# Seven products in place of eight for a graph layer's weights, with the result turned back

## The chip, the core and the metric

The kernel runs on one core of a Trainium2 chip. The metric is the time of one execution on the device in microseconds (us), as the median of several runs. The engines go by the profile's names: PE (TensorE) multiplies matrices and also turns tiles (transposes), DVE (VectorE), ACT (ScalarE) and POOL (GpSimd) work on rows and columns, SP (SyncE) starts the transfers. Matmuls write to PSUM, a small memory of eight banks; everything else is in SBUF. Each engine takes its instructions in a fixed order, the one in which the program issues them, and waits where the data of the next one is not there.

## The reference

The input `x` holds 128 graphs of 64 nodes with 256 features, 8192 rows in all, and `adj` is a 64 x 64 matrix. Four layers follow each other, each with a layer norm and relu ahead and a residual add behind it:

```python
h = jnp.maximum(_layernorm(x, axis=-1), 0.0)
x = x + _L0_gnn_ref(h, adj, ...)      # two graph products with weights, then four window LSTMs
...
x = x + _L1_gnn_ref(h, adj, ...)      # normalised graph product, two weights with batch norms
...
x = x + _L2_gnn_ref(h, L2_gnn_W, adj, L2_gnn_bias)
...
x = x + _L3_gnn_ref(h, adj, L3_gnn_Wqkv, L3_gnn_Wo)   # causal attention over 64 nodes, one head
```

The change is in layer 2, whose three graphs are the diagonal, the upper and the lower part of `adj`, each with a weight of 256 x 256:

```python
def _L2_gnn_ref(x, W, adj, bias):
    adj_0 = jnp.diag(jnp.diagonal(adj))
    adj_1 = jnp.triu(adj, k=1)
    adj_2 = jnp.tril(adj, k=-1)
    h = jnp.einsum('bjf,kfo->kbjo', x, W)
    out = (jnp.einsum('ij,bjo->bio', adj_0, h[0]) + jnp.einsum('ij,bjo->bio', adj_1, h[1])
           + jnp.einsum('ij,bjo->bio', adj_2, h[2]))
    return out + bias[None, None, :]
```

All is in 32-bit floating point.

## The kernel before

The 8192 rows are cut into 16 tiles of 512 rows (`SUP`), each of which lies in SBUF as four groups of 128 rows (`Q`, index `q`), two graphs a group. Layers 0 and 1 run first, over all tiles, since the batch norms need sums over all rows. They leave their result feature-major: features on the 128 partitions in two chunks (`KC`, index `c`), rows along the free axis. The last stage, with layers 2 and 3, is the one that is changed. It takes the tiles in eight pairs of an even tile A and an odd tile B, and the same order of work comes back in every pair.

That order is written by hand. The function `rest` (L1186) holds all the steps of one tile, and each step is entered in a list with a nominal time, `at(t, step, ...)`. `PERIOD` is 52.5 nominal us, and each pair's times are counted from its own start. The list is sorted by time and the steps are issued in that order (at the end of the function), so the nominal times set the order on every engine, and nothing more. A step whose data is late holds up all that stands behind it on its engine. Steps may have times far ahead of the pair's start and so be done within the pair before.

The steps of one tile, in order, with the engine that does each:

- `load` (SP) fetches the rows saved after layer 0. `affine` (L1205, DVE) applies the batch norm's scale and shift in place to the feature-major tile, 128 x 512 for each chunk. `turn` (L1221, PE) transposes to rows, eight transposes a tile, and `turned` (L1224, DVE) adds the residual: `x2`.
- `norm` for layer 2: `stats` (L1235 and L1236, DVE), `root` (L1240 on DVE adds the epsilon, L1241 on POOL raises to the power -1/2), `shift` (L1244, DVE) and `relu` (L1248, ACT): `h2`. Then `biased` (L1261, POOL) adds the layer's bias, spread over all partitions, to `x2`, in four instructions.
- `graphs3` (L1273, PE) multiplies `h2` by the three graphs. It makes `ag`, feature-major, 3 x 512 columns for each of two chunks. A tile has four events of this kind. Each takes two PSUM banks, one for each graph of a group; ACT copies one of them to SBUF and DVE the other (both L1278).
- `weigh` (L1285, PE) is the weight product. For each group of 128 rows it takes 128 x 128 pieces of `ag` as stationary operand and the weights `wl2` as moving one, 256 columns, in 3 x 2 matmuls. A tile has 24 of them. The result has rows on the partitions. `weighed` (L1291, DVE) adds `x2`, which gives `x3`.
- `norm` for layer 3 with the same functions, then `h3` (L1298, PE) and `h3_copy` (L1302, DVE) turn it feature-major: `h3T`.
- Attention: `qsum` (L1313, DVE, four differences), `qproduct` (L1326, PE), `qcopy` (L1330, ACT) and `qadd` (L1333, DVE) make the query side with seven products over halves in place of eight; `hv` (L1350, PE) and `hv_copy` (L1354, ACT) make the values, and `scores` (L1360, PE) the scores. `masked` (L1365, DVE), `largest` (L1370, DVE) and `exps` (L1373, ACT) are the softmax. `turn_e` (L1381, PE), `turned_e` (L1385 and L1386, DVE), `attend` (L1391, PE) and `attended` (L1396, DVE) close the layer, and the rows go out over SP. The last pair has other times and takes the query product directly.

PSUM is one pool of eight banks of 128 x 512 in this stage, and `bank()` gives the next one.

The form in seven products is already in other layers. A product of 2 x 2 blocks is made of seven products of sums of blocks (Strassen's form, in Winograd's variant). `weight_sum` (L309, POOL) makes the four sums of the weights once, `OF` (L297) says which block or sum of the weights belongs to product 1 to 7:

```python
A11, A12, A21, A22, S1, S2, S4 = range(7)
S3 = A21
OF = (None, A11, A12, S4, A22, S1, S2, S3)
...
op(*(w[:, m] for m in ((S1, A21, A22), (S2, S1, A11), (S3, A11, A21), (S4, A12, S2))[k]))
```

Of the kernel before, what the change touches and what calls it, by code (L numbers as in the profile page):

```python
# [20 lines left out]
def kernel(ctx: ExitStack, tc: tile.TileContext, a: dict, out: bass.AP):  # L21
# [615 lines left out]
    def at(t, fn, *args):  # L637
        events.append((t, len(events), fn, args))
# [259 lines left out]
    with tc.tile_pool(name="pz", bufs=1, reuse_waits="tile") as pz:  # L898
# [235 lines left out]
        late = ctx.enter_context(tc.tile_pool(name="late", bufs=1, side="right", reuse_waits="tile"))  # L1134
        adj4 = load_const("adj4", parts_d, [P, 4, P], late)
        adj3, smask = adj4[:, 0:3, :], adj4[:, 3, :]
        wl2 = [weight(f"wl2_{k}", a["W"][k], late) for k in range(3)]
        bl2 = row_bcast("bl2", a["bias"], D, late)
        wqk = late.tile([P, KC, D], F32, tag="wqk", name="wqk")
        aqk = late.tile([P, 7, P], F32, tag="aqk", name="aqk")  # L1140
        wvo = late.tile([P, KC, D], F32, tag="wvo", name="wvo")
        wqkv = weight("wqkv", a["Wqkv"], late)
        wo = weight("wo", a["Wo"], late)

        with tc.tile_pool(name="tp", bufs=2, reuse_waits="tile") as tp_:
            tp.append(tp_)
            emit(1e9)
# [29 lines left out]

    PERIOD, HALF = 52.5, SUP // 2  # L1180
    NP = NS // 2
    with tc.tile_pool(name="pc", bufs=2, reuse_waits="tile") as pc, \
            tc.tile_pool(name="pc1", bufs=1, reuse_waits="tile") as pc1:
        events = []

        def rest(s, at, only_pair, t_T, t_n, t_G, t_W, t_h, t_QH, t_S, t_soft, t_E, t_O, end):  # L1186
# [39 lines left out]
            def norm(src, tag, halves, t_rows, t_relu):  # L1226

                def new():
                    v["st"] = pc.tile([P, Q, 6], F32, tag="ln_st", name="ln_st", bufs=4)
                    v["mv"] = pc.tile([P, Q, 2], F32, tag="ln_mv", name="ln_mv", bufs=4)  # L1230
                    v["rn"] = pc.tile([P, 2, Q], F32, tag="ln_rn", name="ln_rn", bufs=4)
                    v[tag] = pc.tile([P, Q, D], F32, tag=tag, name=tag)

                def stats(q):
                    nc.vector.bn_stats(v["st"][:, q, :], v[src][:, q, :])  # L1235
                    nc.vector.bn_aggr(v["mv"][:, q, :], v["st"][:, q, :])  # L1236

                def root(qs):
                    rn = v["rn"][:, 0, qs]
                    nc.vector.tensor_scalar_add(rn, v["mv"][:, qs, 1], EPS)  # L1240
                    nc.gpsimd.tensor_tensor(rn, rn, mhalf[:, : qs.stop - qs.start], ALU.pow)  # L1241

                def shift(qs):
                    nc.vector.scalar_tensor_tensor(v["rn"][:, 1, qs], v["mv"][:, qs, 0], -1.0,  # L1244
                                                   v["rn"][:, 0, qs], op0=ALU.mult, op1=ALU.mult)

                def relu(q):
                    nc.scalar.activation(v[tag][:, q, :], v[src][:, q, :], AF.Relu,  # L1248
                                         bias=v["rn"][:, 1, q : q + 1], scale=v["rn"][:, 0, q : q + 1])

                at(t_rows[0] - 0.01, new)
                for q in range(Q):
                    at(t_rows[q // 2] + 0.6 * (q % 2), stats, q)
                for k, qs in enumerate((q2s(0), q2s(1)) if halves else (slice(0, Q),)):
                    at(t_relu[k] - 1.5, root, qs)
                    at(t_relu[k] - 0.1, shift, qs)
                    for q in range(qs.start, qs.stop):
                        at(t_relu[k] + 0.6 * (q - qs.start), relu, q)

            def biased(q):  # L1260
                nc.gpsimd.tensor_add(v["x2"][:, q, :], v["x2"][:, q, :], bl2)  # L1261

            def graphs3(c, k):

# [12 lines left out]
                    to = v["ag"][:, c, :, 2 * k * P : (2 * k + 2) * P]  # L1277
                    copy(to.rearrange("p k (q n) -> p q k n", q=2)[:, :, :, b * T : (b + 1) * T], half[b])  # L1278

            def weigh(k, q):  # L1280
                if q == 0:
                    v["W"] = two(bank())
                for n in range(3 * KC):
                    c, m = divmod(n, 3)
                    nc.tensor.matmul(v["W"][:, q, :], v["ag"][:, c, m, ts(2 * k + q, P)],  # L1285
                                     wl2[m][:, c, :], start=(n == 0), stop=(n == 3 * KC - 1))

            def weighed(k):
                if k == 0:
# [29 lines left out]
            def qproduct(name, j):  # L1319
                new = ("q", name) not in v  # L1320
                if new:
                    v["q", name] = bank()[:, :HALF]
                if "qk" not in v:
                    v["qk"] = pc1.tile([P, KC, SUP], F32, tag="qk", name="qk")
                x_ = (b_(0, 0), b_(1, 0), b_(1, 1), *(v["t"][:, k] for k in (4, 1, 2, 3)))[j - 1]
                nc.tensor.matmul(v["q", name], aqk[:, OF[j], :], x_, start=new,  # L1326
                                 stop=(name, j) in (("a", 4), ("b", 3), ("c", 2)), skip_group_check=True)
# [84 lines left out]
                at(t_T + 0.1 * k + 0.01, turned, k)  # L1412
            if first_:
                norm("x2", "h2", True, (t_T + 0.455, t_T + 1.8), (t_T + 3.2, t_T + 4.6))
                for q in range(Q):
                    at(t_T + 7 + 0.7 * q, biased, q)
            else:
                norm("x2", "h2", False, (t_n, t_n + 1.2), (t_n + (11.9 if s % 2 and s > 1 else 4.1),))
                for q in range(Q):
                    at(t_n + (18 if s % 2 else 10.5) + 0.7 * q, biased, q)  # L1420
# [47 lines left out]
        for i in range(NP):  # L1468
            t0, first_, end = PERIOD * i, i == 0, i == NP - 1

            def at(t, fn, *args, t0=t0):
                events.append((t0 + t, len(events), fn, args))

            rest(2 * i, at, i, -8.6 if first_ else -40.2, -38.3, 0, (7.0, 12.6), 29.0, 32.6, 40.0, 42.7,
                 46.3 if end else 48.46, 50.4 if end else 50.85, False)
            if first_:
                at(-7.6, weight_product, 2, wo, wvo)
                for k in range(8):
                    at(3.0 + 0.5 * k, qk_weights, k)
            rest(2 * i + 1, at, i, -3.0 if first_ else -27.6, 1.5 if first_ else -25.4, 12.3 if first_ else 3.5, (17.8, 26.5), 39.1,  # L1480
                 (42.0, 45.4, 48.7, 49.6, 52.1) if end else 42.0, 46.7 if end else 48.9,
                 49.5 if end else 59.5, 53.0 if end else 64.7, 53.8 if end else 75.6, end)
        for _, _, fn, args in sorted(events, key=lambda e: e[:2]):
            fn(*args)
    new_banks()
# [38 lines left out]
```

## Time and profile before

| what | value |
|---|---|
| median of 3 runs (lowest to highest) | 1876.81 us (1876.74 to 1877.57) |
| the profiled execution | 1876.78 us |
| its span | 1875.1 us |
| PE busy | 1853.9 us, 99% of the span |
| DVE, ACT, POOL busy | 1129.4, 925.7, 645.4 us |
| one period of the last stage | 50.88 us |
| of that PE, DVE, ACT, POOL busy | 50.88, 36.58, 20.23, 10.09 us |
| weight product L1285 | 768 matmul records |

The profile is of one execution. A 32-bit matmul appears as two records, so the 24 matmuls of 16 tiles are 768. The chain of waits is followed from the last instruction back to whatever let each step start. An engine's share of the chain is thus the part of the time that it set itself. A timeline gives start and length of each instruction or of several alike in a row, and in square brackets how long the engine stood idle before it and what ended that.

### The profile page before, as it was taken

To read this page: it belongs to the slowest core of one execution; us is meant where nothing else is said; L and a number is where in the kernel's file an instruction comes from. 1 tells how busy PE (TensorE), PEld (TensorE's weight loads), DVE (VectorE), ACT (ScalarE), POOL (GpSimd) and SP (SyncE) were. 2 spreads that over 40 slices of the span, in tenths; PEclk is the share of its full clock that TensorE was granted. 3 is DMA by queue.
4 is the path that set the end of the run, shared out by engine and by line. 5 is a ranking of instruction groups with operands and counts; after the bars stand their busy time and mean duration, and the time that the engine had idled before them with its cause. 6 is when DMAs were issued, how large, how long until landed. Compare 5 with 4: busy or idle time off the path is not lost.

```text
span 1875.1 us, 19841 instructions
## 1 busy us (share of the span) xinstructions
PE 1853.9 (99%) x7080; PEld 1168.8 (62%) x7080; DVE 1129.4 (60%) x2254; ACT 925.7 (49%) x1594; POOL 645.4 (34%) x553
## 2 busy tenths in 40 slices
PE   8999999999999999999999999999999999999999
PEld 7997444444445666666444444566444788888887
DVE  6775777634546435445633333588876776667674
ACT  6776666534435334433533333378685434433442
POOL 4451422443424433422442222267353412211220
PEclk9999999999999999999999999999999999999999
DMA  4110001000001000000000000243200111111101
GB/s 146 57 57 1 1 1 29 16 1 0 1 0 45 1 0 1 1 1 1 23 0 0 1 0 0 102 132 116 71 1 2 44 46 46 35 46 46 46 23 34
DMA packets 50642, 54.86 MB, mean 29 GB/s; under 512 B 3184, under 2 KB 45936, under 8 KB 50544
## 3 DMA queue, kind: packets, MB, share of 16 engines
q1 hardware_dynamic: 50096, 53.30, 8.9%
q8 instruction: 56, 0.92, 0.2%
q14 instruction: 42, 0.34, 0.1%
q10 hardware_dynamic: 448, 0.30, 0.0%
HBM read 36.55 MB, written 17.04 MB: 29 GB/s over the span
## 4 chain that ended last, share of the span: by engine, by line
PE 93%; DVE 3%; POOL 1%; ACT 1%; DMA 1%; issue 1%; SPq 0%; ACTq 0%; DVEq 0%; POOLq 0%
PE ps L686 34%; PE ps L692 19%; PE ps L1285 8%; PE ps L930 5%; PE ps L1047 4%; PE ps L1350 3%; PE ps L392 3%; PE ps L402 3%; PE ps L1326 2%; PE ps L431 2%; PE ps L1273 2%; PE ps L1360 2%; PE ps L1391 1%; PE ps L623 1%; PE ps L1298 1%; PE ps L579 1%
## 5 line engine op out<-in xcount | busy, mean ns | idle before, releaser
L708 DVE TENSOR_TENSOR gate<-gate,ps 128x512 f32<-128x512 f32 (+2 forms) x378 | 223.9, 620 | 449.0 <-PE ps L692 367.7
L686 PE MATMUL ps<-tx,wih 128*128 128x512 f32 (+2 forms) x996 | 441.2, 541 | 1.9 <-ACT gate L711 1.0
L686 PE MATMUL ps<-hT,wih 128*128 128x512 f32 (+2 forms) x756 | 338.5, 541 | 0.0
L711 ACT COPY gate<-ps 128x512 f32<-128x512 f32 (+2 forms) x252 | 134.5, 534 | 378.4 <-PE ps L692 325.4
L686 PEld LDWEIGHTS ps<-tx,wih 128*128 128x128 f32 x996 | 188.4, 190 | 188.2 <-issue 128.2
L704 ACT ACTIVATE gate<-gate,lbias 128x512 f32<-128x512 f32 (+2 forms) x252 | 216.7, 860 | 160.0 <-DVE gate L708 160.0
L692 PE MATMUL ps<-h,whh 128*128 128x512 f32 (+2 forms) x576 | 256.6, 527 | 0.0
L686 PEld LDWEIGHTS ps<-hT,wih 128*128 128x128 f32 x756 | 143.6, 190 | 141.6 <-issue 79.4
L692 PE MATMUL ps<-th,whh 128*128 128x512 f32 (+2 forms) x432 | 192.5, 527 | 0.0
L731 POOL TENSOR_TENSOR gate<-gate 128x1024 f32<-128x1024 f32 (+2 forms) x36 | 71.9, 2019 | 297.5 <-ACT gate L704 297.5
L1285 PE MATMUL ps<-wl,ag 128*128 128x256 f32 x768 | 172.1, 380 | 0.0
L692 PEld LDWEIGHTS ps<-h,whh 128*128 128x128 f32 x576 | 109.4, 190 | 100.2 <-issue 76.5
L1285 PEld LDWEIGHTS ps<-wl,ag 128*128 128x128 f32 x768 | 143.4, 190 | 20.2 <-ACT ag L1278 1.8
L731 POOL TENSOR_TENSOR cell<-gate 128x1024 f32<-128x1024 f32 (+2 forms) x36 | 79.4, 2225 | 174.8 <-ACT gate L704 174.8
L1241 POOL TENSOR_TENSOR ln_rn<-ln_rn,mhalf 128x4 f32<-128x4 f32 (+1 forms) x33 | 32.8, 995 | 300.8 <-DVE ln_rn L1240 300.3
L692 PEld LDWEIGHTS ps<-th,whh 128*128 128x128 f32 x432 | 82.1, 190 | 75.2 <-issue 57.4
L1248 ACT ACTIVATE h<-x,ln_rn 128x256 f32<-128x256 f32 x128 | 68.2, 593 | 103.3 <-DVE ln_rn L1244 103.3
L731 POOL TENSOR_TENSOR cell<-gate,cell 128x1024 f32<-128x1024 f32 (+2 forms) x31 | 62.8, 2044 | 110.2 <-ACT gate L704 110.2
L711 DVE COPY gate<-ps 128x512 f32<-128x512 f32 (+2 forms) x126 | 78.6, 624 | 20.8 <-PE ps L692 20.8
L704 ACT ACTIVATE gate<-ps,lbias 128x512 f32<-128x512 f32 (+2 forms) x126 | 79.6, 631 | 3.8 <-PE ps L692 1.0
L736 ACT ACTIVATE gate<-cell 128x1024 f32<-128x1024 f32 (+2 forms) x72 | 68.0, 951 | 26.1 <-POOL cell L731 26.1
L648 DVE TENSOR_TENSOR tx<-hT,tx 128x512 f32<-128x512 f32 (+2 forms) x70 | 57.7, 825 | 13.8 <-PE ps L686 10.2
(236 smaller groups left out, 2933.8 us busy)
## 6 DMA issues: line engine op xcount, KB each, us to landing
xt<-in_x_dram SPq DMA_DIRECT2D x30, 512.0 KB, 4.2
x1d<-xt SPq DMA_DIRECT2D x16, 512.0 KB, 3.0
x<-x1d SPq DMA_DIRECT2D x16, 512.0 KB, 4.9
out_dram<-x SPq DMA_DIRECT2D x15, 512.0 KB, 3.0
wih<-in_WihT_dram SPq DMA_DIRECT2D x16, 256.0 KB, 4.8
whh<-in_WhhT_dram SPq DMA_DIRECT2D x12, 256.0 KB, 4.8
xt<-in_x_dram SPq DMA_DIRECT2D x6, 128.0 KB, 3.2
wl<-in_W_dram SPq DMA_DIRECT2D x3, 256.0 KB, 3.6
```

Source lines behind the costliest of these rows:

```text
L648: yield nc.vector.tensor_sub(t[k], *((b[1][0], b[0][0]), (b[1][1], t[0]), (b[1][1], b[1][0]), (b[0][1], t[1 % len(t)]))[k])
L686: nc.tensor.matmul(wide(p_[:, :N]), wih[0][:, OF[k], gi, :], x_, start=first_, stop=(j == 0), skip_group_check=True)
L692: nc.tensor.matmul(p_[:, :N], whh[0][:, OF[k], gi, :], h_, start=False, stop=True, skip_group_check=True)
L704: nc.scalar.activation(to, r[bank_][:, :N] if bank_ else to, fn, bias=lbias[:, l, m : m + 1])
L708: nc.vector.tensor_add(slot(n, hc), slot(n, hc), r[bank_][:, :N])
L711: op(slot(n, hc), r[bank_][:, :N])
L731: fn(*((t["G"] if isinstance(t, dict) and "G" in t else st["c"])[:, n, :, : st["N"]] for t in tiles))
L736: nc.scalar.activation(o_, c, AF.Tanh)
L930: nc.tensor.matmul(r[name], con["w1"][:, OF[j], g, :], x_, start=new, stop=(name, j) in (("a", 4), ("b", 3), ("c", 2)), skip_group_check=True)
L1047: nc.tensor.matmul(banks[name], w2[:, OF[j], k, :], x_, start=(new and k == 0), stop=(k == 1), skip_group_check=True)
L1248: nc.scalar.activation(v[tag][:, q, :], v[src][:, q, :], AF.Relu, bias=v["rn"][:, 1, q : q + 1], scale=v["rn"][:, 0, q : q + 1])
L1285: nc.tensor.matmul(v["W"][:, q, :], v["ag"][:, c, m, ts(2 * k + q, P)], wl2[m][:, c, :], start=(n == 0), stop=(n == 3 * KC - 1))
```

## The change

Layer 2's weight product is taken the other way round and in seven products. The weights become the stationary operand and `ag` the moving one, in two halves of 256 columns (rows of the tile), so that the result is feature-major, 2 x 2 blocks: output chunk `o` by half `n`. A tile then has 7 x 3 matmuls of 256 columns. Tile 0 takes a direct product with the same operands, 24 matmuls (`gdirect`).

The steps that come with it: `gsum` makes the four sums of blocks of `ag`, 128 x 768 each, on POOL, two of them in place. `gevict` (ACT) brings four products from PSUM to SBUF and adds the bias, which is a column per output chunk in this layout; `gadd` (DVE) adds the other three from PSUM. `turn_back` (PE) transposes the result to rows, eight transposes, and `weighed` then adds `x2` as before. `biased` goes. The weights `wl2` are loaded in four pieces instead of three, with four weight sums on POOL.

PSUM is split into a pool of three banks for the products (those of the queries too) and one of five for the rest. The differences `qsum` move from DVE to POOL. In `norm` the shift of two operands on DVE is replaced by a product with -1 on DVE and a small product on POOL. Many nominal times change, among them the next tiles' turn (A -40.2 to -14.5, B -27.6 to -37.2) and B's end of the attention (64.7 to 67.35, 75.6 to 79.5).

```diff
-        wl2 = [weight(f"wl2_{k}", a["W"][k], late) for k in range(3)]
-        bl2 = row_bcast("bl2", a["bias"], D, late)
+        wl2 = late.tile([P, 7, 3, P], F32, tag="wl2", name="wl2")
+        for o in range(2):
+            for c in range(2):
+                nc.sync.dma_start(wl2[:, 2 * o + c], a["W"].rearrange(
+                    "m (c p) (o n) -> o c p m n", c=2, o=2)[o, c])
+        bl2 = load_const("bl2", a["bias"].rearrange("(c p) -> p c", p=P), [P, KC], late)
...
+        for k in range(4):
+            if k != 2:
+                at(B + 60 + 5.16 * k, weight_sum, wl2, k)
...
+    new_banks(abc=3, psum=5)
...
-                    rn = v["rn"][:, 0, qs]
+                    rn, nm = v["rn"][:, 0, qs], v["rn"][:, 1, qs]
                     nc.vector.tensor_scalar_add(rn, v["mv"][:, qs, 1], EPS)
+                    nc.vector.tensor_scalar_mul(nm, v["mv"][:, qs, 0], -1.0)
                     nc.gpsimd.tensor_tensor(rn, rn, mhalf[:, : qs.stop - qs.start], ALU.pow)
-
-                def shift(qs):
-                    nc.vector.scalar_tensor_tensor(v["rn"][:, 1, qs], v["mv"][:, qs, 0], -1.0,
-                                                   v["rn"][:, 0, qs], op0=ALU.mult, op1=ALU.mult)
+                    nc.gpsimd.tensor_mul(nm, nm, rn)
...
-            def biased(q):
-                nc.gpsimd.tensor_add(v["x2"][:, q, :], v["x2"][:, q, :], bl2)
...
-            def weigh(k, q):
-                if q == 0:
-                    v["W"] = two(bank())
-                for n in range(3 * KC):
-                    c, m = divmod(n, 3)
-                    nc.tensor.matmul(v["W"][:, q, :], v["ag"][:, c, m, ts(2 * k + q, P)],
-                                     wl2[m][:, c, :], start=(n == 0), stop=(n == 3 * KC - 1))
+            def g_(c, n):
+                return v["ag"][:, c, :, ts(n, HALF)]
+
+            def gsum(k):
+                if k == 0:
+                    v["t2"] = late.tile([P, 3 * KC, D], F32, tag="wT", name="tg")
+                t1, t2 = v["t2"][:, 0:3], v["t2"][:, 3:6]
+                if k == 0:
+                    nc.gpsimd.tensor_sub(t1, g_(0, 1), g_(0, 0))
+                elif k == 1:
+                    nc.gpsimd.tensor_sub(g_(0, 1), g_(1, 1), g_(0, 1))
+                elif k == 2:
+                    nc.gpsimd.tensor_add(t2, g_(0, 1), g_(0, 0))
+                else:
+                    nc.gpsimd.tensor_sub(g_(1, 0), g_(1, 0), t2)
+
+            def gproduct(name, j):
+                new = ("g", name) not in v
+                if new:
+                    v["g", name] = bank("abc")[:, :HALF]
+                x_ = (g_(0, 0), g_(1, 0), g_(1, 1), g_(1, 0), v["t2"][:, 0:3] if j == 5 else None,
+                      v["t2"][:, 3:6] if j == 6 else None, g_(0, 1))[j - 1]
+                for m in range(3):
+                    nc.tensor.matmul(v["g", name], wl2[:, OF[j], m, :], x_[:, m], start=new and m == 0,
+                                     stop=m == 2 and (name, j) in (("a", 4), ("b", 3), ("c", 2)),
+                                     skip_group_check=True)
...
+            def gevict(o, n, name):
+                if "y2" not in v:
+                    v["y2"] = late.tile([P, KC, 3 * D], F32, tag="wqkv", name="y2")
+                nc.scalar.activation(w_(o, n), v["g", name], AF.Identity, bias=bl2[:, o : o + 1])
+
+            def gadd(o, n, name):
+                nc.vector.tensor_add(w_(o, n), w_(o, n), v["g", name])
+
+            def turn_back(k):
+                v["W"] = two(bank())
+                for q in range(2):
+                    for c in range(KC):
+                        nc.tensor.transpose(v["W"][:, q, ts(c, P)], v["y2"][:, c, ts(2 * k + q, P)], ident)
...
-                nc.vector.tensor_sub(t[:, k], *(None, (b_(0, 1), b_(0, 0)), (b_(1, 1), t[:, 1]),
+                nc.gpsimd.tensor_sub(t[:, k], *(None, (b_(0, 1), b_(0, 0)), (b_(1, 1), t[:, 1]),
                                                 (b_(1, 1), b_(0, 1)), (b_(1, 0), t[:, 2]))[k])
...
-                    v["q", name] = bank()[:, :HALF]
+                    v["q", name] = bank("abc")[:, :HALF]
...
+            if first_:
+                for k in range(4):
+                    at(t_W[k], gdirect, k // 2, k % 2)
+            else:
+                for t, (name, j) in zip(t_W, (("c", 2), ("a", 1), ("b", 5), ("a", 6), ("b", 3), ("a", 7), ("a", 4))):
+                    at(t, gproduct, name, j)
+                for t, fn, *args in ((1, gevict, 0, 0, "a"), (2, gevict, 1, 1, "b"), (3, gevict, 0, 1, "a"),
+                                     (6, gevict, 1, 0, "a"), (4, gadd, 0, 1, "b"), (5, gadd, 1, 1, "a")):
+                    at(t_W[t] + 1.35, fn, *args)
+                at(t_W[1] + 1.8, gadd, 0, 0, "c")
+                for k in range(4):
+                    at(t_sums[k], gsum, k)
             for k in range(2):
-                for q in range(2):
-                    at(t_W[k] + 2.6 * q, weigh, k, q)
-                at(t_W[k] + 5.3, weighed, k)
-            norm("x3", "h3", False, (t_W[0] + 5.8, t_W[1] + 5.8), (t_W[1] + 8.8,))
+                at(t_Y[k], turn_back, k)
+                at(t_Y[k] + 0.5, weighed, k)
+            norm("x3", "h3", False, (t_Y[0] + 0.7, t_Y[1] + 0.7), (t_relu3,))
```

The nominal times of a pair, as they are in the changed version (in the order of `rest`'s arguments; the old ones are in the listing above):

```diff
+            rest(2 * i, at, i, -8.6 if first_ else -14.5, -12.5, 0,
+                 (7.0, 9.6, 12.2, 14.8) if first_ else (7.0, 8.3, 9.6, 10.9, 12.2, 13.5, 16.1),
+                 (3.3, 5.2, 7.1, 9.0), (17.4, 19.15) if first_ else (19.15, 17.4), 23.56, 26.1, 31.4, 40.0, 42.7,
+                 46.3 if end else 48.46, 50.4 if end else 50.85, False)
...
+            rest(2 * i + 1, at, i, -3.0 if first_ else -37.2, 1.5 if first_ else -35.8,
+                 12.3 if first_ else 3.5, (17.85, 19.6, 20.9, 22.2, 23.5, 24.8, 29.65),
+                 (16.0, 17.0, 18.0, 22.0) if first_ else (12.3, 14.2, 16.1, 22.0), (32.2, 30.95), 35.3, 39.1,
+                 (42.0, 45.4, 48.7, 49.6, 52.1) if end else 42.0, 46.7 if end else 48.9,
+                 49.5 if end else 59.5, 53.0 if end else 67.35, 53.8 if end else 79.5, end)
```

More of the change, by code (lines that the diff above doesn't have):

```diff
@@ L1184, with rest @@
         events = []
-        def rest(s, at, only_pair, t_T, t_n, t_G, t_W, t_h, t_QH, t_S, t_soft, t_E, t_O, end):
+        def rest(s, at, only_pair, t_T, t_n, t_G, t_W, t_sums, t_Y, t_relu3, t_h, t_QH, t_S, t_soft, t_E, t_O, end):
             first_, v = s == 0, {}
@@ L1249, in relu @@
                                          bias=v["rn"][:, 1, q : q + 1], scale=v["rn"][:, 0, q : q + 1])
-                at(t_rows[0] - 0.01, new)
+                at(min(t_rows) - 0.01, new)
                 for q in range(Q):
@@ L1255, in norm @@
                     at(t_relu[k] - 1.5, root, qs)
-                    at(t_relu[k] - 0.1, shift, qs)
                     for q in range(qs.start, qs.stop):
                         at(t_relu[k] + 0.6 * (q - qs.start), relu, q)
-            def biased(q):
-                nc.gpsimd.tensor_add(v["x2"][:, q, :], v["x2"][:, q, :], bl2)
             def graphs3(c, k):
@@ new lines, in gdirect, with w_ @@
+            def gdirect(n, o):
+                v["g", o] = bank("abc")[:, :HALF]
+                for c in range(KC):
+                    for m in range(3):
+                        nc.tensor.matmul(v["g", o], wl2[:, 2 * o + c, m, :], g_(c, n)[:, m],
+                                         start=(c == 0 and m == 0), stop=(c == KC - 1 and m == 2))
+                gevict(o, n, o)
+            def w_(o, n):
+                return v["y2"][:, o, ts(n, HALF)]
+            def gevict(o, n, name):
+                if "y2" not in v:
+                    v["y2"] = late.tile([P, KC, 3 * D], F32, tag="wqkv", name="y2")
+                nc.scalar.activation(w_(o, n), v["g", name], AF.Identity, bias=bl2[:, o : o + 1])
@@ L1288, in weighed @@
+            def gadd(o, n, name):
[3 more added lines that the diff above has]
+                for q in range(2):
+                    for c in range(KC):
+                        nc.tensor.transpose(v["W"][:, q, ts(c, P)], v["y2"][:, c, ts(2 * k + q, P)], ident)
             def weighed(k):
-                if k == 0:
+                if "x3" not in v:
                     v["x3"] = pc.tile([P, Q, D], F32, tag="x3", name="x3", bufs=4)
@@ L1414, in rest @@
                 norm("x2", "h2", True, (t_T + 0.455, t_T + 1.8), (t_T + 3.2, t_T + 4.6))
-                for q in range(Q):
-                    at(t_T + 7 + 0.7 * q, biased, q)
-            else:
-                norm("x2", "h2", False, (t_n, t_n + 1.2), (t_n + (11.9 if s % 2 and s > 1 else 4.1),))
-                for q in range(Q):
-                    at(t_n + (18 if s % 2 else 10.5) + 0.7 * q, biased, q)
+            else:
+                norm("x2", "h2", False, (t_n, t_n + 1.2), (t_n + (4.1 if s == 1 else 8.9 if s % 2 else 7.5),))
             for k in range(4):
                 at(t_G + 0.8 * k, graphs3, *((k % 2, k // 2) if first_ else (k // 2, k % 2)))
+            if first_:
[10 more added lines that the diff above has]
+                    at(t_sums[k], gsum, k)
             for k in range(2):
-                for q in range(2):
-                    at(t_W[k] + 2.6 * q, weigh, k, q)
-                at(t_W[k] + 5.3, weighed, k)
-            norm("x3", "h3", False, (t_W[0] + 5.8, t_W[1] + 5.8), (t_W[1] + 8.8,))
+                at(t_Y[k], turn_back, k)
+                at(t_Y[k] + 0.5, weighed, k)
+            norm("x3", "h3", False, (t_Y[0] + 0.7, t_Y[1] + 0.7), (t_relu3,))
             for c in range(KC):
@@ L1472, in at @@
                 events.append((t0 + t, len(events), fn, args))
-            rest(2 * i, at, i, -8.6 if first_ else -40.2, -38.3, 0, (7.0, 12.6), 29.0, 32.6, 40.0, 42.7,
+            rest(2 * i, at, i, -8.6 if first_ else -14.5, -12.5, 0,
+                 (7.0, 9.6, 12.2, 14.8) if first_ else (7.0, 8.3, 9.6, 10.9, 12.2, 13.5, 16.1),
+                 (3.3, 5.2, 7.1, 9.0), (17.4, 19.15) if first_ else (19.15, 17.4), 23.56, 26.1, 31.4, 40.0, 42.7,
                  46.3 if end else 48.46, 50.4 if end else 50.85, False)
@@ L1477 @@
                 at(-7.6, weight_product, 2, wo, wvo)
+                at(17.0, weight_sum, wl2, 2)
                 for k in range(8):
-                    at(3.0 + 0.5 * k, qk_weights, k)
-            rest(2 * i + 1, at, i, -3.0 if first_ else -27.6, 1.5 if first_ else -25.4, 12.3 if first_ else 3.5, (17.8, 26.5), 39.1,
+                    at(20.5 + 0.5 * k, qk_weights, k)
+            rest(2 * i + 1, at, i, -3.0 if first_ else -37.2, 1.5 if first_ else -35.8,
+                 12.3 if first_ else 3.5, (17.85, 19.6, 20.9, 22.2, 23.5, 24.8, 29.65),
+                 (16.0, 17.0, 18.0, 22.0) if first_ else (12.3, 14.2, 16.1, 22.0), (32.2, 30.95), 35.3, 39.1,
                  (42.0, 45.4, 48.7, 49.6, 52.1) if end else 42.0, 46.7 if end else 48.9,
-                 49.5 if end else 59.5, 53.0 if end else 64.7, 53.8 if end else 75.6, end)
+                 49.5 if end else 59.5, 53.0 if end else 67.35, 53.8 if end else 79.5, end)
         for _, _, fn, args in sorted(events, key=lambda e: e[:2]):
```

## Prediction

> **What bounds the kernel now.** I read first the engines' shares, then the chain that ended last, then the windows of three consecutive periods of the last stage (a period is one pair of tiles), then the timelines of DVE, ACT and POOL inside one of them.
>
> ```profile
> PE 1853.9 (99%) x7080; PEld 1168.8 (62%) x7080; DVE 1129.4 (60%) x2254; ACT 925.7 (49%) x1594; POOL 645.4 (34%) x553
> ...
> PE 93%; DVE 3%; POOL 1%; ACT 1%; DMA 1%; issue 1%; SPq 0%; ACTq 0%; DVEq 0%; POOLq 0%
> ...
> 1614.55:1665.43 50.88, 50.88 (x309) 45.46 (x308) 36.58 (x95) 20.23 (x52) 10.09 (x12) 1.00 0.13 42
> ```
>
> PE (TensorE) is the bound, and in the stage that changes it is never idle: the window of 50.88 us has 50.88 us of PE. So a matmul taken out of this stage is worth its full time, and every wait put into PE's order costs its full time. DVE is at 72% of the period, POOL at 20%: average room, but what counts is who is late at which place. The chain in order of time gives the durations on PE, one line for one run of work (start, us, matmul records):
>
> ```profile
> 1601.33 1.08 PE ps L1298 x8
> ...
> 1614.62 5.40 PE ps L1273 x64
> 1620.03 5.38 PE ps L1285 x24
> 1625.40 0.44 PE ps L1381 x4
> 1625.84 0.87 PE ps L1221 x8
> 1626.71 10.36 PE ps L1285 x48
> ```
>
> One tile's weight product is 48 records in 10.36 us: 24 matmuls of two passes, 0.432 us each. Eight transposes are 0.87 us, or 1.08 where they wait 0.2 for a relu (first line). The graph products of the pair's two tiles (L1273) are 8 events, 5.40 us, 0.65-0.7 each, first four of the even tile A, then four of the odd tile B; each event fills two PSUM banks, one emptied by ACT, one by DVE.
>
> **What the Trainium skill says.** (1) "GPSIMD Engine Reference", section 8 "Key points": GpSimd shares its SBUF interface with VectorE, and the two collide when VectorE works in a two-port mode or reads two SBUF inputs. The trace agrees, see below. (2) "VectorE: DVE Perf Modes", "Mode 2×_2P": fp32 tensor_scalar and copies from SBUF to SBUF may use both ports; an operand in PSUM excludes it. The trace fits: the affine step L1205, 512 elements, takes 0.528 us, a reduction of as many (L1370) 0.684. (3) "PSUM — Partial Sum Buffer": eight banks of 2 KiB a partition, not reachable from GpSimd. So the new sums over `ag` can be on POOL, the adds from PSUM cannot.
>
> **The change, part by part.** The sum is made against the profiled execution, 1876.78 us (span 1875.1 and 1.7 around it); the median, 1876.81, is the same.
>
> *PE.* Per tile seven products of three matmuls, 21 instead of 24, all of 256 columns: 3 x 0.432 = -1.30. The turning back adds 8 transposes: +0.87. Net -0.43 a tile, -0.85 a pair; the 0.2 of the odd tile's wait may go too. Supertile 0 keeps 24 matmuls and pays the transposes. Whole: 15 x -0.43 + 0.87 = -5.6. This is all the change can win, 0.3%: 1871.2.
>
> *POOL.* New are four sums of 128x768 a tile. No such shape is in the trace; from POOL's 256 elements in 0.73 and 512 in 1.27 the line 0.19 + 2.11 ns an element gives 1.81 each, 7.2 in a row. Bounds: 1.7 (slope of the last step) and 2.1 (with collisions as in L1037, 1.53 for 512). The bias adds leave (4 x 0.78 a tile), the four differences of the query product come (4 x 0.73). So POOL goes from 10.1 to about 25 us of a period, at most half busy: not a bound by its sum.
>
> *ACT and DVE.* ACT gains four evictions of 128x256 from PSUM with bias (0.37 each, price of L1330), DVE three adds a tile (0.42, L1333) and loses four differences (0.54 and 0.64) and the shift (0.31). DVE's load thus falls slightly. ACT's Identity is already used at L1202 and costs no new table.
>
> *Weights.* Four DMAs instead of three, four sums on POOL (0.73 to 1.3 each), three of them in gaps of up to 4.6 us that POOL has in the stage before. I take 0; without that cover up to 1 each, +3.
>
> *Moved steps.* The next tiles' load, affine steps and turning (L1221) move: A's from 40 to 14.5 nominal us ahead of its pair, B's from 27.6 to 37.2. The load, one DMA on SP, stays 8 us ahead of the turning and lands in 4.9 (issue table): hidden, at most nothing lost unless a buffer is held. The transposes cost PE the same in the new place. B's attention end moves 2.65 and 3.9 us later, between products that need PE anyway: 0. But the affine steps of a later B now come in A's product stretch, those of the next A beside the query differences: S2 and S4.
>
> *Banks: S1.* Eight banks become five for general use and three for the products. The graph product takes two per event, so the third event needs a bank that the first has given back. Its start is due 1.3 after the first's; DVE's copy of the first ends 1.5 after it (timeline: 1615.55 + 0.56 is 1616.11, the chain has the start at 1614.62). From there ACT's copies (0.48, and 0.17 until it starts again) set a cycle of about 1.48 for two events instead of 1.30. Over the eight events, with A's first bank wait, +1.0; bounds 0 (if the copies run closer when pressed) and 1.2. Queued behind: the first seven products, attended's banks.
>
> *Port: S2, the main cost.* Count from the graph product's start, 1614.62. A's last copy lands at 2.8, and POOL works its four sums from 2.9 to about 10.4. In the same stretch DVE has, in its order, copies of the odd tile B, two affine steps for a tile to come, then the maximum of another tile, upon which ACT makes four exponentials, and only then the eviction of the finished product "a", on which PE's next product in the same bank (a, 6) waits. DVE's line-up today:
>
> ```profile
> 1618.20 0.54 DVE L1205 TENSOR_SCALAR hT<-hT,co 128x512 f32<-128x512 f32 x1
> 1618.65 0.55 DVE L1278 COPY ag<-ps 128x384 f32<-128x384 f32 x1
> 1619.12 0.54 DVE L1205 TENSOR_SCALAR hT<-hT,co 128x512 f32<-128x512 f32 x1
> 1619.57 1.48 DVE L1278 COPY ag<-ps 128x384 f32<-128x384 f32 x3
> 1620.96 0.68 DVE L1370 TENSOR_REDUCE mx<-sc 128x4 f32<-128x512 f32 x1
> ```
>
> The affine step goes SBUF to SBUF, the two-port kind. What POOL does to such an instruction the trace shows once in layer 1 (DVE, POOL):
>
> ```profile
> 1300.73 1.27 POOL L835 TENSOR_TENSOR T<-ag 128x512 f32<-128x512 f32 x1 [4.04 <-PE ps L930]
> ...
> 1301.39 0.64 DVE L607 TENSOR_SCALAR ln_rn<-ln_mv 128x4 f32<-128x4 f32 x1
> 1301.95 0.16 DVE L608 TENSOR_SCALAR ln_rn<-ln_mv 128x4 f32<-128x4 f32 x1
> ```
>
> A 0.16 us instruction takes 0.64 and ends when POOL's operation ends (1302.0): it is held for the whole rest of it. With sums of 1.81 us back to back (ends at 4.7, 6.5, 8.3), the first affine step comes at 6.96 (as today behind B's copies, later by S1), waits for the third sum's end, 8.3, and ends 8.7; the fourth sum slips in and holds the second affine step to about 10.8; the maximum ends 11.4; four exponentials at a pitch of 0.39 end 13.1 and the eviction 13.5. PE wants product (a, 6) at 10.3. Stall about 3.3 a period; bounds: 0.5 (only the order on ACT, no hold) and 3.4; 1.6 if one step alone is held. Behind the waiting products stands all of PE, as it runs in order.
>
> *S3, S4.* The even tile's third layer norm is now turn_back, add, statistics, power and product on POOL, four relus: its h3 is late by about 0.4 (power 1.0 and the small product 0.2 are on POOL's queue). The query differences are on POOL (4 x 0.73 instead of DVE's 4 x 0.6) beside the next A's two affine steps, ahead of the odd tile's h3 and scores: 0.4. Bounds 0 and 1 each.
>
> *First and last pair.* The first: +0.87 - 0.43 and POOL's queue with four more weight sums before the power, about +0.3 (-0.3 to 1.4). The last has no affine steps, so S1 alone: +0.2.
>
> **Sum.** 50.88 - 0.85 - 0.2 + 1.0 + 3.3 + 0.4 + 0.4 = 54.9 a period, +4.0; with half the unsure S3, S4 and a little overlap among stalls (a wait behind another wait is not paid twice) +3.5. Six steady pairs: +21; first and last +0.5. 1876.8 + 21.5 = 1898.
>
> **The rivals.**
> - *One hold alone*: affine steps fall between two sums, or POOL's fourth sum waits for DVE instead: 1.6 for 3.3, so about +2 a pair, 1888. For it: in the trace DVE also holds POOL (0.39 for 0.19 once, L888).
> - *Banks alone, no hold*: the layer 1 row was chance, POOL and DVE share by turns as in the differences L1313 (0.94 beside POOL's L1261, 0.41 alone). Then S1 +1.0 and S2 0.5 against -1.05, with S3 and S4 partly: +0.6 a pair, 1881; same to slightly slower.
> - *All hidden, faster*: POOL's sums come off DVE's way, ACT and DVE copies keep up with five banks. Then PE gets its 0.43 a tile: 1871.2. For it: DVE is 72% and POOL half busy, and DVE's load falls. It decides where the sum of new stalls in a pair is under 0.85; since PE has no idle time at all, a single hold suffices to lose this. Against it: the ACT order alone eats half.
> - *Worse*: the holds also hit the root's small tensor_scalars of the odd tile, or B's products wait for its sums as well: up to 2 more a pair, 1910.
> That the change doesn't do what it says I exclude: the seven products and the removed 24 are in the diff.
>
> **How the numbers follow.** Both steps held 0.48 (1893-1904), one 0.15 (1884-1892), banks alone 0.12 (1876-1883), hidden 0.20 (1870-1874), worse 0.05. A measurement of this kernel tells 0.2%, 3.75 us, from no change. Faster by more 0.20; within it 0.10 (most of the banks case); slower 0.70. Both signs hold weight, so the range reaches from 1871 (half the hidden case) to 1905; the likeliest case's own is 1893 to 1904.
>
> **What would show it.** Right: an affine step of about 1.7 us instead of 0.53 that ends with a POOL sum; PE's idle time of 2 to 3 us before the product (a, 6), put down to ACT's eviction; the graph product of a tile at 5.7 to 6 us instead of 5.4; period near 54.5. S1 wrong: graph product still 5.4. S2 wrong: affine steps at 0.53, the exponentials beginning within 8 us of the graph product's start. S3 wrong: no PE wait before h3. My forecast falls as a whole if the period is under 50.9; if the period is right and the total is not, the first pair or the weights are to blame.

## The result and the profile after

| | before | changed |
|---|---|---|
| median of 4 runs (lowest to highest) | 1876.78 us (1876.62 to 1877.57) | 1895.57 us (1895.50 to 1896.83) |
| profiled execution, its span | 1876.78, 1875.1 us | 1895.62, 1893.7 us |
| one steady period of the last stage | 50.88 us | 53.58 us |

The ratio is 1.0101 with a 95% interval of 1.0088 to 1.0114: the changed kernel is slower by 18.8 us, where 21.5 was forecast. Where those are lost is read in the same order as before. First the engines' shares and two windows of the changed kernel, each one pair of tiles long (columns: window, length, then busy time and instructions of PE, PE's weight loads, DVE, ACT and POOL, then the clock granted to PE, DMA share, GB/s):

```profile
PE 1859.7 (98%) x7118; PEld 1168.6 (62%) x7118; DVE 1125.1 (59%) x2239; ACT 952.5 (50%) x1658; POOL 761.4 (40%) x646
```

```profile
1567.79:1621.37 53.58, 51.49 (x314) 44.98 (x313) 36.42 (x93) 23.56 (x60) 25.09 (x24) 1.00 0.12 40
1514.31:1567.79 53.48, 51.39 (x313) 44.95 (x312) 36.39 (x93) 23.55 (x60) 25.08 (x24) 1.00 0.13 40
```

PE was never idle in a period; now it is for 2.1 us of each. No other engine is near its limit: DVE's load is the same, 36.4 us, and POOL's 25.1 is what the sum gave. So it is waits, not an engine that is too full. Which waits they are, the list of PE's waits says for the whole last stage (us in total, times, the longest):

```profile
PE ps L1307 <- ACT y L1325: 10.8, 6, 2.0
PE ps L1346 <- ACT h L1254: 2.9, 17, 0.3
PE ps L1275 <- ACT h L1254: 1.5, 1, 1.5
```

L1307 is the new weight product, L1325 the eviction, L1346 is h3 (L1298 before) and L1254 the relu (L1248 before). The first line is the forecast wait: six times, once in each steady pair, a product waits for an eviction on ACT. The third line is no new loss: the last stage's first graph product waited for a relu before too, 1.81 us. PE's own timeline of one period, start and length of each run of matmuls, shows the place:

```profile
1567.79 5.97 PE L1275 MATMUL ps<-adj,h 64*128 64x192 f32 x64
1573.70 2.86 PE L1307 MATMUL ps<-ag,wl 128*128 128x256 f32 x12
1576.39 1.46 PE L1307 MATMUL ps<-tg,wl 128*128 128x256 f32 x6
1579.61 1.53 PE L1307 MATMUL ps<-tg,wl 128*128 128x256 f32 x6 [1.76 <-ACT y L1325]
1580.98 2.75 PE L1307 MATMUL ps<-ag,wl 128*128 128x256 f32 x12
...
1594.83 0.66 PE L1346 MATMUL ps<-ident,h 128*128 128x128 f32 x3
1595.65 0.77 PE L1346 MATMUL ps<-ident,h 128*128 128x128 f32 x5 [0.16 <-ACT h L1254]
1596.26 1.89 PE L1439 MATMUL ps<-hw,eT 128*128 128x256 f32 x8
```

The graph product runs from 1567.79 to 1573.70, 5.91 us where it was 5.40. Then come the products c2 and a1 (12 records), b5 (6; the letter stands for the PSUM bank that a product is added to, the number for the product), and a hole of 1.76 us ahead of a6 (6 records). Since the timeline counts a last record to its modelled end, a step is best measured from start to start: b5 takes 3.22 us (1576.39 to 1579.61), of which 1.30 are its own. h3 takes 1.43 from 1594.83 to 1596.26 instead of 0.87. Why a6's eviction is late, DVE, POOL and ACT show in the same stretch:

```profile
1573.81 0.56 DVE L1280 COPY ag<-ps 128x384 f32<-128x384 f32 x1
1574.28 0.54 DVE L1213 TENSOR_SCALAR hT<-hT,co 128x512 f32<-128x512 f32 x1
1574.73 2.04 DVE L1213 TENSOR_SCALAR hT<-hT,co 128x512 f32<-128x512 f32 x1
1576.69 0.67 DVE L1418 TENSOR_REDUCE mx<-sc 128x4 f32<-128x512 f32 x1
```

```profile
1572.70 1.81 POOL L1294 TENSOR_TENSOR ag<-ag 128x768 f32<-128x768 f32 x1
1574.59 1.90 POOL L1296 TENSOR_TENSOR tg<-ag 128x768 f32<-128x768 f32 x1
1576.57 1.88 POOL L1298 TENSOR_TENSOR ag<-ag,tg 128x768 f32<-128x768 f32 x1
```

```profile
1577.46 0.40 ACT L1421 ACTIVATE sc<-sc,mx 128x128 f32<-128x128 f32 x1 [3.36 <-DVE mx L1418]
...
1579.01 0.81 ACT L1325 ACTIVATE y<-ps,bl 128x256 f32<-128x256 f32 x2
```

The first affine step slips in at its usual 0.54 us as the second sum ends. The second begins with the third sum, is held through it (1574.59 to 1576.49) and ends at 1576.77. The maximum follows, then the first exponential at 1577.46, after ACT has stood idle for 3.36 us, and then the evictions at 1579.01. It is the chain of the forecast, link by link, with one step held instead of two. Not every step of DVE is held: the maximum takes 0.67 us beside the fourth sum, and before, with no sum beside it, 0.68.

A steady period therefore adds up as follows, start to start: the seven products and the turning back -0.85, graph product +0.51, b5 with the wait for a6 and a6's slow start +2.0, h3 A +0.56, h3 B 1.45 instead of 1.08 +0.37, scores +0.09. That is 2.7, as the windows say. (The first products take 0.10 more than their matmuls alone, but that is no loss of the change: before, the 24 records behind the graph product took 5.29 us from start to start, and 24 records alone 5.18.) The period is paid six times (+16.3 from the first steady graph product to the last pair's, 321.62 us for 305.29). The last pair's graph product starts 57.77 us before the end instead of 57.02, +0.75. The rest, 1.5, lies in the first pair: its graph product starts at 1461.29 us, before at 1461.46, so what is new ahead of it, the weights and their sums, cost nothing.

### The profile page after: what moved, and what is told of

Read it like the earlier page. It is cut to its first block, busy times and chain, and to the rows that moved or that the text cites. A ratio compares the mean times of both kernels' runs of the same rounds, so it can differ in the third digit from the quotient of the medians.

```text
span 1893.7 us, 20227 instructions
## 1 busy us (share of the span) xinstructions
PE 1859.7 (98%) x7118; PEld 1168.6 (62%) x7118; DVE 1125.1 (59%) x2239; ACT 952.5 (50%) x1658; POOL 761.4 (40%) x646
## 5 line engine op out<-in xcount | busy, mean ns | idle before, releaser
L1307 PE MATMUL ps<-ag,wl 128*128 128x256 f32 x450 | 106.7, 381 | 0.2 <-DVE y L1328 0.2
L1307 PEld LDWEIGHTS ps<-ag,wl 128*128 128x128 f32 x450 | 83.2, 191 | 11.8 <-issue 1.9
L1254 ACT ACTIVATE h<-x,ln_rn 128x256 f32<-128x256 f32 x128 | 67.5, 591 | 24.1 <-POOL ln_rn L1251 24.1
L1325 ACT ACTIVATE y<-ps,bl 128x256 f32<-128x256 f32 x64 | 29.4, 469 | 99.7 <-PE ps L1307 95.9
```

Source lines behind the costliest of these rows:

```text
L1307: nc.tensor.matmul(v["g", name], wl2[:, OF[j], m, :], x_[:, m], start=new and m == 0, stop=m == 2 and (name, j) in (("a", 4), ("b", 3), (" ...
L1325: nc.scalar.activation(w_(o, n), v["g", name], AF.Identity, bias=bl2[:, o : o + 1])
```

## The experiments

Two theories are set against each other. The one of the prediction, **port**: a POOL sum over two SBUF operands holds a two-port step of DVE until it ends. Its rival, **order**: ACT and DVE simply have too much ahead of the eviction, and POOL's sums play no part.

### The sums in two pieces

```diff
-                    nc.gpsimd.tensor_sub(t1, g_(0, 1), g_(0, 0))
...
+                for r in range(2):
+                    op(to[:, :, ts(r, P)], x[:, :, ts(r, P)], y_[:, :, ts(r, P)])
```

The diff shows one of the four sums; all four are split. Nothing else changes, and POOL has a little more to do.

> Each of POOL's four block sums is issued as two sums of 128x384; same work, same place in the queue. Theory 'port' (a sum over two SBUF operands on POOL holds DVE's two-port affine step until its end, and the delay runs over the maximum, the exponentials and the eviction to product (a, 6)): the hold gets shorter with the piece; the longest affine step falls from 2.04 to 1.1-1.5 us, PE's wait before (a, 6) from 1.76 to 0.9-1.3, the time from 1895.6 to 1889.5-1893. Rival 'order' (ACT and DVE are simply too full ahead of the eviction, POOL's sums play no part): no change, 1895-1897, the affine step as long as before.

Measured: 1891.24 us (ratio to the kernel before 1.0074, 1.0059 to 1.0089). The longest affine step is 1.22 us, PE's wait before a6 1.10:

```profile
L1213 DVE TENSOR_SCALAR hT<-hT,co x24: 534/882/1220, 1520.1 to 1809.6; 128x512 f32<-128x512 f32 x24
```

(minimum, median and maximum in ns; in the changed kernel they were 533, 934 and 2040). The hold is as long as the piece. In the changed kernel the second affine step ended 0.28 to 0.29 us after the end of the third sum in each of the six steady pairs; here both steps end 0.28 to 0.29 us after the end of the piece that was running when they began, again in each of the six. A step that was only slowed by sharing would not keep that distance to sums of 1.9 and of 1.0 us. A mere lack of room on ACT or DVE would not have cared about the pieces, so *order* alone falls.

```profile
1577.63 1.53 PE L1304 MATMUL ps<-tg,wl 128*128 128x256 f32 x6 [1.10 <-POOL ag L1295]
```

The view puts a6's wait down to POOL's fourth sum in this kernel. That is a near tie: the sum ends at 1577.54, and DVE's add that waits for the same eviction as a6 starts at 1577.52. The product doesn't read that sum: in the last pair of this kernel b5 and a6 run without a gap from 1839.62 to 1842.21, while the fourth sum runs until 1841.74.

### The affine steps on ACT

```diff
-                if s == 1:
+                if s:
                     nc.scalar.activation(y[c], y[c], AF.Identity, bias=co2[:, 1, c : c + 1],
```

> The affine steps go from DVE to ACT (Identity with scale and bias, 0.81 us each instead of 0.53), at the same nominal times. Theory 'port': ACT isn't held by POOL; though ACT now has 1.6 us more ahead of the exponentials, the maximum comes 1.8 earlier, the wait before (a, 6) falls from 1.76 to 0-0.3, and the odd tile's h3 comes some 0.2-0.4 earlier: 2.0 a period, 1882-1885. Rival 'order': more work on ACT ahead of the eviction makes the wait longer, 1.8-3.3 a period, 1895-1904.

Measured: 1881.04 us (1.0020, 1.0012 to 1.0028), a period of 51.08, a little better than *port* expected. The wait before a6 is gone, though ACT has 1.5 us more to do just ahead of the exponentials:

```profile
1572.54 1.52 ACT L1210 ACTIVATE hT<-hT,co 128x512 f32<-128x512 f32 x2
1573.96 0.39 ACT L1421 ACTIVATE sc<-sc,mx 128x128 f32<-128x128 f32 x1
...
1575.50 0.46 ACT L1325 ACTIVATE y<-ps,bl 128x256 f32<-128x256 f32 x1
```

The graph product of this period starts at 1566.34, so the eviction comes 9.2 us after it instead of 11.2. The wait for h3 B went too: 0.96 us from its start to the scores' instead of 1.45. In the first pair a turning back waits 1.31 us for ACT, as tile 2's two steps stand ahead of an eviction there.

### The maximum ahead of the affine steps

```diff
-                 49.5 if end else 59.5, 53.0 if end else 67.35, 53.8 if end else 79.5, end)
+                 49.5 if end else 58.75, 53.0 if end else 67.35, 53.8 if end else 79.5, end)
```

> The odd tile's maximum moves on DVE from behind the two affine steps to ahead of them; nothing else moves. Theory 'port': the affine steps are still held (about 2 us for the longer), but the maximum no longer stands behind them: the exponentials start at about 7.3 us after the graph product's start instead of 9.7, the wait before (a, 6) falls from 1.76 to 0-0.3, 1884-1886. If what is late were not the held affine step but the graph product's copies or POOL's sums themselves: the wait stays above 1.2, 1892-1896.

Measured: 1883.25 us (1.0032, 1.0021 to 1.0044), 51.58 a period: 2.0 less, all of the wait and of a6's slow start. DVE, POOL and PE in this kernel:

```profile
1572.41 0.67 DVE L1418 TENSOR_REDUCE mx<-sc 128x4 f32<-128x512 f32 x1
1573.00 3.78 DVE L1213 TENSOR_SCALAR hT<-hT,co 128x512 f32<-128x512 f32 x2
...
1572.73 1.81 POOL L1296 TENSOR_TENSOR tg<-ag 128x768 f32<-128x768 f32 x1
1574.62 1.88 POOL L1298 TENSOR_TENSOR ag<-ag,tg 128x768 f32<-128x768 f32 x1
...
1574.52 2.75 PE L1307 MATMUL ps<-tg,wl 128*128 128x256 f32 x12
```

The two affine steps take 3.78 us together and end at 1576.78, 0.28 us after the fourth sum. So here both are held, and it costs PE nothing: b5 and a6 are one run of 12 records without a gap, since nothing urgent stands behind the steps. The size of S2 is thus measured: 2.0 us a period.

### One PSUM pool

```diff
-    new_banks(abc=3, psum=5)
+    new_banks(psum=8)
...
-                    v["g", name] = bank("abc")[:, :HALF]
+                    v["g", name] = bank()[:, :HALF]
```

(and the same in `gdirect` and `qproduct`)

> One PSUM pool of eight banks again for all, otherwise as changed. Theory 'banks' (with five banks the graph product waits for copies): a pair's graph products fall from 5.9 to 5.4 us and the first products by 0.1, the wait before (a, 6) stays at 1.8; about 0.6 a pair in eight pairs, 1890-1892. Rival (the copies are slower for another reason, POOL's sums for example): graph products stay at 5.9, 1895-1896.

Measured: 1899.03 us (1.0115, 1.0098 to 1.0132). Both theories missed. The graph products do take 5.4 us again, so the banks had made them longer; but the time rose by 3.5. PE's timeline, two of the six places:

```profile
1524.95 1.53 PE L1307 MATMUL ps<-tg,wl 128*128 128x256 f32 x6 [2.17 <-ACT y L1325]
1578.25 2.62 PE L1307 MATMUL ps<-tg,wl 128*128 128x256 f32 x6 [2.24 <-ACT y L1325]
```

What was saved ahead of a6 came back as a longer wait for the same eviction. And the same six records take 2.62 us where they took 1.53. The granted clock over the six us from each place tells why, and for the second place in two shorter windows:

```profile
1524.95:1530.95 6.00, 6.00 (x34) 5.42 (x35) 2.56 (x7) 0.69 (x2) 4.08 (x3) 1.00 0.01 3
1578.25:1584.25 6.00, 6.00 (x22) 4.98 (x23) 0.88 (x3) 0.69 (x2) 3.07 (x2) 0.72 0.00 0
...
1578.55:1581.96 3.41, 3.41 (x10) 2.69 (x9) 0.01 (x1) 0.47 (x1) 0.85 (x1) 0.50 0.00 0
1581.96:1585.37 3.41, 3.41 (x23) 3.13 (x22) 1.68 (x5) 0.00 (x0) 3.25 (x3) 1.00 0.00 0
```

The clock is 0.72 in the mean: it is 0.50 for 3.41 us and then 1.00 again, and PE gets through 22 records instead of 34. It is so behind four of the six waits; each such period is 1.7 us longer (55.0 against 53.3). To tell whether the pool or the length of the wait was to blame, the next kernel joins the one pool with the split sums.

> One PSUM pool of eight, and POOL's block sums in two pieces each. With one pool alone the time rose to 1899.0, and the profile had TensorE's clock at about half for 3.4 us behind four of six waits of 2.2 to 2.5 us before (a, 6). Theory (the shorter graph product only lengthens that wait, and the rise is the clock's answer to the length of the wait, not the pool's doing): the pieces keep the wait at 1.4-1.8 us, the clock stays at 1.00 throughout, 1888.5-1890.5. Rival (the one pool itself costs time in the products): the products stay slow behind (a, 6), the mean clock below 0.999, above 1893.

Measured: 1888.55 us (1.0062, 1.0045 to 1.0079), the wait 1.53 to 1.60 (put down to POOL's fourth sum again, the same near tie), the clock 1.000. So the one pool does not by itself slow the clock, and a wait of under 1.8 us left the clock alone in every period of three kernels. To see the bank saving itself, the wait has to be out of the way:

> Two edits together: the maximum ahead of the affine steps, and one PSUM pool of eight. In the run with one pool alone the graph product became 0.5 us shorter, but the wait before (a, 6) grew by as much. Theory 'banks are real, but hidden behind the hold': with the hold off the path the 0.5-0.6 a pair comes out in full, 1883.2 falls to 1878-1880. Rival (the one pool costs something else that took the gain): 1883-1886.

Measured: 1877.35 us (1.0002, 0.9993 to 1.0010), 5.9 less than with the maximum ahead alone and slightly more than expected; 50.84 a period instead of 51.58. The bank split costs 0.74 a pair: 0.50 in the graph product, the rest at h3 B (1.31 for 1.45) and the scores (1.79 for 1.89). Most of it had been hidden behind a6's wait: with one pool alone, the two periods without a slow clock were only 0.3 shorter (53.3 for 53.58).

### What is left: h3

Each of the following kernels has one pool. The first takes the affine steps of tiles 3 and up to ACT and puts the first of the odd tile's two attend steps ahead of the even tile's h3 on PE; the second stays behind it:

```diff
-                if s == 1:
+                if s == 1 or s > 2:
...
-                 49.5 if end else 59.5, 53.0 if end else 67.35, 53.8 if end else 79.5, end)
+                 49.5 if end else 59.5, 53.0 if end else 67.35, 53.8 if end else 78.4, end)
```

> Affine steps on ACT (but for tile 2), one PSUM pool, and the odd tile's attend of the pair before goes ahead of the even tile's h3 on PE instead of behind it. Theory (the even tile's h3 comes 0.56 late because its norm chain does, and any 1.7 us of other PE work ahead of it covers this): the wait before h3 A goes, period 51.08 - 0.55 - 0.56 = 49.9-50.1, the time 1871.5-1875, below the kernel before. Rival (what covers h3 makes the next product wait for h3's copies): period 50.4 or more, 1876-1879.

Measured: 1871.83 us, ratio 0.9973 (0.9962 to 0.9983): faster than the kernel before, by 5.0 us. Its window:

```profile
1563.18:1613.14 49.96, 49.96 (x313) 44.60 (x312) 32.33 (x89) 26.35 (x64) 24.99 (x24) 1.00 0.14 43
```

PE's timeline has attend at 1587.83, h3 A at 1588.70 and attend at 1589.57, so 0.87 us of other work ahead of h3 A are enough, where the expectation has 1.7. PE is never idle again, and the period is shorter than before by 0.92: the 0.85 of the arithmetic and the old wait of 0.2, less 0.13 that one product still loses.

The second moves the odd tile's layer-2 statistics and relus behind the even tile's layer-3 root instead:

```diff
-            rest(2 * i + 1, at, i, -3.0 if first_ else -37.2, 1.5 if first_ else -35.8,
+            rest(2 * i + 1, at, i, -3.0 if first_ else -37.2, 1.5 if first_ else -29.5,
...
-(t_n + (4.1 if s == 1 else 8.9 if s % 2 else 7.5),)
+(t_n + (4.1 if s == 1 else 5.0 if s % 2 else 7.5),)
```

> Affine steps on ACT (but for tile 2), one PSUM pool, and the odd tile's layer-2 statistics (2.3 us of DVE for a relu that isn't due for half a period) go from ahead of the even tile's layer-3 statistics to behind its root. Theory (h3 A is late because DVE takes those statistics first): the wait before h3 A goes, 49.9-50.2 a period, and the first pair's wait of 2 us shrinks too: 1870.5-1874.5. Rival (the chain turn back, add, power, relu is itself too long): the wait stays at 0.4-0.6, 1875-1877.

Measured: 1875.35 us (0.9992, 0.9984 to 1.0000), 50.71 a period. h3 A no longer waits, so the statistics had been what made it late. The power and the small product on POOL were left as they were, so they alone do not make it. But the relus that come with the statistics now stand on ACT, mixed with two affine steps, ahead of an eviction, and the turning back waits for that (0.53 idle in PE's timeline). One wait was traded for another, and so the time is in the rival's range, though the wait that the rival expected to stay is gone. With both edits:

> All edits of the two kernels ahead together: affine steps on ACT (but for tile 2), one pool, attend ahead of h3 A, the odd tile's statistics later. If both only cover the same wait of 0.56: as the better of the two, 1870.5-1874. If each still leaves a part: 0.2 a period better than either.

Measured: 1875.33 us (0.9990, 0.9982 to 0.9998), the same as the second alone. The better of the two or a little less was expected; both missed, as the new wait of the later relus stays and decides.

The last kernel leaves the affine steps on DVE, with the maximum ahead of them, and is otherwise the first:

> As the kernel with affine steps on ACT, one pool and attend ahead of h3, but with the affine steps left on DVE and the maximum ahead of them. It tells what the affine steps on DVE still cost beside POOL's query differences. Theory (they are held there too, and through the layer-3 statistics of the odd tile its h3 comes late): the odd tile's h3 keeps its waits of about 0.37 a period against the version on ACT, 50.3 a period, 1873.5-1875. Rival (h3 B's wait came from the DVE order alone, or is covered now): 49.9-50.0 a period, 1871.5-1872.5.

Measured: 1877.62 us (1.0003, 0.9995 to 1.0012), 50.91 a period. Both expectations missed: it is worse than either. DVE in one period:

```profile
1592.05 0.86 DVE L1444 SCALAR_TENSOR_TENSOR x<-ps,mx,x 128x256 f32<-128x256 f32 x2
1592.84 1.40 DVE L1213 TENSOR_SCALAR hT<-hT,co 128x512 f32<-128x512 f32 x2
1594.16 0.67 DVE L1339 TENSOR_TENSOR x<-x,ps 128x512 f32<-128x512 f32 x1
```

The affine steps of the next even tile take 1.40 us beside POOL's query differences, where two alone take about 1.0 (0.45 apart, the last 0.54), and they stand ahead of the odd tile's adds and statistics. PE waits for a query add (0.35 idle) and for h3 B. So S4 is real: the first of the three kernels has the steps on ACT and differs besides only in the maximum's place, and its period is 49.96, 0.95 less. The hold makes the steps about 0.4 us longer; how much of the 0.95 is due to it, and how much to the steps' own place on DVE, no run separates. Against the kernel with the maximum ahead and one pool (1877.35), the only difference is the attend step, and alone it gains nothing: the wait for h3 A goes, and the one for the query add comes.

## Why the prediction was right

**PE.** The net saving of 0.85 a pair is confirmed: with the waits gone (one attend step ahead, affine on ACT, one pool) the kernel takes 1871.8 us; the sum for "all hidden" was 1871.2. There the rival of the other side came true, only not in the kernel as changed.

**S2, the port.** The mechanism and its place were right: held by POOL's sum, the affine step delays maximum, exponentials and eviction, and a6 waits. Splitting the sums, moving the maximum and moving the steps each removed their part of it. The size was off: 2.0 us instead of 3.3. The step of the working that failed is "the first affine step comes at 6.96, waits for the third sum's end". It came at 6.5, ahead of the third sum, so one step was held, as in the rival "one hold alone" (1.6 there). The working had put S1's delay on it, but DVE's last copy ended at 6.6 us after the graph product's start, hardly later than before (6.5). The place in time decided: with the maximum ahead the first step came at 7.1, both were held, and the second ended at 10.9, which are the working's own 6.96 and 10.8.

The Trainium skill ("GPSIMD Engine Reference", section 8 "Key points") speaks of contention between the two engines; these traces say what form it takes here: the two-port step is not slowed but held, for what is left of POOL's instruction.

**S1, banks.** Right in kind, 0.5 to 0.74 a pair instead of 1.0, but not additive: next to S2 it was hidden, as the graph product's end mostly sets how long a6 waits. The 1.48 us for two events doesn't follow from the working's own numbers: 0.48 and 0.17 are 0.65 a copy, 1.30 for two, which is the old pitch. In the trace ACT's copies of the pair at 1567.79 start 0.65 to 0.67 apart, as before, but for two gaps of 0.83 and 0.77: two late copies, not a slower cycle.

**S3, S4.** h3 A 0.56 for 0.4. Its cause was other than stated: not the power and the small product on POOL, but the odd tile's layer-2 norm, whose statistics stand ahead on DVE: with that moved behind and the POOL work left in place, the wait went, while one pool alone or the affine steps on ACT alone had left it there. h3 B net +0.37 for +0.2; 0.14 of it went with the bank split, and all of it with the affine steps on ACT (0.96 from start to start).

**First and last pair.** +1.5 and +0.75 for +0.3 and +0.2. In the first pair h3 A alone ends 1.65 us late; the whole is just above the upper end that was given, 1.4. In the last pair the graph product takes 0.5 longer, a wait for an add on DVE costs 0.4, and h3 B takes 1.62 for 0.87; against that stand the 0.85 saved. The working had S1 alone there.

So the total is close partly by luck, as errors cancel: the steady pairs gave 2.7 instead of 3.5 (-4.7 in all), the two ends 1.8 more. The likeliest case, both steps held, is not what happens in the steady period; the time of the case that does happen was put at 1888, too low for the ends and for h3.

## What to carry to other kernels

Where PE has no idle time, price a saving of a few tenths against the waits it opens: here 0.85 us saved cost 3.6 in the other places. Before giving POOL long two-operand sums, look what two-port steps DVE has in that stretch, and what stands behind them; keep the urgent short work ahead of such steps, give them to ACT, or cut the sums into pieces. When one wait hides another, removing the hidden one alone shows nothing or a loss; remove the one that ends last first.

## What was not expected of the hardware

A wait of PE can change what comes after it: behind four of six waits of 2.2 to 2.5 us the granted clock was 0.50 for 3.41 us (1.7 us lost each), while behind waits of 1.76 us or less it never was, and behind one of 2.02 and two of 2.17 and 2.25 it was not either. The Trainium skill ("TensorE: Matmul & The Clock Gate", "Part 1: The HAM clock gate") has the clock halve after an idle window of about 3.4 us; here idle times well below that were enough at times.

Which waits it hits has a pattern in the kernel with one pool alone. The four stretches at half clock begin at 1578.55, 1633.16, 1742.39 and 1797.00 us. They lie 54.61, 109.23 and 54.61 us apart, which is 16, 32 and 16 times their own length of 3.413 us, as if the clock were set on a fixed beat of that length. If that beat is laid over the waits, the beat just ahead of each slow stretch holds 2.24, 2.14, 2.24 and 2.52 us of PE's idle time. The two waits that left the clock alone are cut by the beat, into 1.15 and 1.02 us and into 1.80 and 0.45 us. So it fits all six that the idle time within one beat counts, with a limit somewhere between 1.80 and 2.14 us. This was worked out afterwards, from one execution, and no run tested it.

The hold goes both ways: POOL's third sum took 1.90 us beside an affine step that had begun ahead of it, and 1.81 where none had; with one pool and the maximum ahead it took up to 2.09. And an eviction from PSUM with a bias on ACT took 0.47 us for 256 columns, a plain copy 0.37, which was the price that the prediction took for it.
